# Four graph layers on one core: layer 0's weights as the stationary operand, layer 1 in a written order, one tile moved from matrix to list

## The chip, the core and the metric

The kernel runs on one core of a Trainium2 chip. The metric is the time on the device in microseconds (us). The core's engines work in parallel, each through its own queue in order: TensorE (PE, with its weight loads PEld), VectorE (DVE), ScalarE (ACT), GpSimd (POOL) and SyncE (SP). SBUF is the working memory of 128 partitions, PSUM the memory that matmuls write to.

## The reference, cut to what matters

There are B = 8 batches of N = 2048 nodes with D = 64 values each and one adjacency matrix of 2048 x 2048, in which a node has few neighbours. Four layers follow each other, each as `x = layernorm(x + layer(x, adj))`.

```python
# layer 0: attention with a score that is a sum of two parts
h = layernorm((x * nw + nb + x) @ W) * g0 + b0
e = leaky_relu(s1[:, :, None] + s2[:, None, :], 0.2)      # s1 = h.a1, s2 = h.a2
att = softmax(where(adj > 0, e, -big)); out = elu(att @ h + h)
# layer 1: a softmax over neighbours for each of the 64 values by itself
feat = softplus(x * w0 / sqrt(2) + b0); scores = feat * wa + ba
out[i] = sum_j adj exp(scores[j]) feat[j] / sum_j adj exp(scores[j])
# layer 2: mean over the neighbours, two weight matrices, relu, layernorm
# layer 3: four attention heads and an output head, layernorm
```

## The kernel before, in words

Nodes lie in NT = 16 tiles of 128; a tile holds a node's 8 x 64 values as one row of 512. The preparation (L360 to L425) reads the adjacency matrix tile by tile and makes two forms of it. For the first DENSE = 8 tiles of receiving nodes it makes the matrix `ET` in fp8, transposed by PE (L367 to L372). For all tiles it makes lists: `src`, the sending nodes of each edge in 5 windows of 128 edges for each of two groups of 64 nodes, and the selections `SelT` and `Sel`, which say which edge belongs to which node. `node_products` (L287) computes layer 0's products, normalises them into `H` and writes them to the table `htab0` in device memory. In `H` the first value of each batch is replaced by the neighbour's part of the score; it is recovered later from the fact that the values of a norm add to nothing (L494).

**Layer 0's loop** (L514 to L532) stands under a manual schedule: PE, ACT, DVE and POOL keep the order of the program. `fetch` issues ten indirect DMAs (gathers, L204) for a tile, each fetching the rows of 128 edges, and has PE bring the receiver's part of the score to the edges (`pe`, L451). `weights` adds both parts, takes the leaky maximum and two Exps. `weigh` multiplies the gathered rows by their weights on DVE (L472, five products of 128x1024), and PE adds them up with the selection as stationary operand (L478, 512 columns moving) and the weights beside them into `pd` (L480). `divide`, `combine`, `activate` and `normalise` follow one to three turns later.

**Layer 1** first makes its rows (`make_rows`, L571): exp(score) and its product with the feature, 1024 values per node, written to `rtab` (L587) and split in three bf16 pieces `R` (L589 to L593, on POOL, DVE, ACT and POOL). Tiles 0 to 7 are summed by matrix: `add_rows` (L598) multiplies `ET` by the pieces, six matmuls per pair of tiles (L601), the first FIRST = 3 tiles while the rows are made. Then tiles 15 down to 8 are summed by list: `fetch` (L637) gathers rows of 4 KB from `rtab`, `add_edges` (L646) sums them (L656), in three quads of four, four and two gathers per tile, spread between the matrix steps of tiles 3 to 7 by the condition at L672. `finish` (L607) divides (L610), adds to X and norms pairs of tiles. A planner orders what stands under no manual schedule.

**Layer 2** turns all rows (L803 to L821), then sums in the same two ways: matrix tiles with three matmuls per pair (L978), list tiles by gathers from `ytab` and L958, under a manual schedule with POOL copying finished tiles (`show`, L901). `by_list` and `by_matrix` follow DENSE (L796, L932), so the change reaches into this layer too. Layer 3 follows: the heads (gathers `xs`, weights at L1083) and the output head, which sums with weights as the stationary operand (L1420); both use lists alone and don't depend on DENSE.

Of the kernel before, what the change touches and what calls it, by code (L numbers as in the profile page):

```python
# [48 lines left out]
def kernel(ctx: ExitStack, tc: tile.TileContext, ins: dict, out: bass.AP):  # L49
# [150 lines left out]
    DENSE = 8  # L200
# [23 lines left out]
    htab0 = dram.tile([N + 1, BD], F32, name="htab0")  # L224
    no_row(htab0)
    l0 = ExitStack()
    wp = l0.enter_context(tc.tile_pool(name="l0w", bufs=1))
    H = wp.tile([P, NT, BD], F32, name="H")
# [33 lines left out]
    for k, a in enumerate((a1, a2)):  # L262
# [5 lines left out]
        if k:  # L268
            first_col = wp.tile([P, 2], F32, name="first_col")
            nc.vector.tensor_copy(first_col, Wv[:, :, 0])  # L270
            nc.vector.tensor_copy(Wv[:, :, 0], Wa[:, 1])
            nc.vector.tensor_copy(Wa[:, 1], first_col)

# [13 lines left out]
    def node_products(t0, wk, ps):  # L287
# [4 lines left out]
        for q in range(HALF):  # L292
# [14 lines left out]
            nc.vector.tensor_reduce(var[:, q], sq[:, :, 1:], AX.X, ALU.add)  # L307
            held.append(ph)
        v4, r4, t4 = (a.rearrange("p q (a k) -> p q a k", k=2) for a in (var, rstd, tmp))
        nc.vector.tensor_tensor(t4, pq[:, :, :, 1], pq[:, :, :, 1], ALU.mult)  # L310
        nc.vector.tensor_tensor(var, var, tmp, ALU.add)
        nc.vector.scalar_tensor_tensor(var, var, 1.0 / D, eps.unsqueeze(2).to_broadcast(var.shape), op0=ALU.mult, op1=ALU.add)
        inv_sqrt(*(a.rearrange("p q b -> p (q b)") for a in (rstd, var, tmp)))
        for q, ph in enumerate(held):
            t = t0 + q
            nc.vector.tensor_tensor(H[:, t].rearrange("p (b d) -> p b d", d=D),
                                    ph.rearrange("p a (k d) -> p (a k) d", d=D), along(rstd[:, q]), ALU.mult)
            nc.sync.dma_start(htab0[t * P:(t + 1) * P, :], H[:, t])
# [111 lines left out]

    wk = l0.enter_context(tc.tile_pool(name="l0k", bufs=2))
    ps_e = l0.enter_context(tc.tile_pool(name="l0pse", bufs=2, space=PSUM))
    ps_o = l0.enter_context(tc.tile_pool(name="l0pso", bufs=3, space=PSUM))
    ps_w = l0.enter_context(tc.tile_pool(name="l0psw", bufs=1, space=PSUM))
    held, zs, stats = {}, {}, {}

    def fetch(it):
        hs = wk.tile([P, GS * NG, B, D], F32, name="hs")
        for s in range(GS):
            for g in range(NG):  # L440
                gather(hs[:, s * NG + g].rearrange("p b d -> p (b d)"), htab0, it, s, g)
        selTf = wk.tile([P, GE], F32, name="selTf")
        nc.scalar.activation(selTf, SelT[:, it], AF.Copy)  # L443
        self_ = wk.tile([P, NG, NQ, GB], F32, name="self_")
        nc.scalar.activation(self_, Sel[:, it], AF.Copy)
        s1g = wk.tile([P, NG, B], F32, name="s1g")
        nc.vector.tensor_tensor(s1g, S1[:, it].unsqueeze(1).to_broadcast(s1g.shape),
                                group.unsqueeze(2).to_broadcast(s1g.shape), ALU.mult)
        pe = ps_e.tile([P, GS, NG * B], F32, name="pe")
        for s in range(GS):  # L450
            nc.tensor.matmul(pe[:, s], selTf[:, s * P:(s + 1) * P], s1g.rearrange("p g b -> p (g b)"), start=True, stop=True)  # L451
        held[it] = hs, self_, pe

    def weights(it):
        hs, self_, pe = held[it]
        wm = wk.tile([P, GS * NG, B], F32, name="wm")
        nc.vector.tensor_tensor(wm, pe.rearrange("p s (g b) -> p (s g) b", b=B), hs[:, :, :, 0], ALU.add)
        w = ps_w.tile([P, GS * NG, B], F32, name="w")
        nc.vector.scalar_tensor_tensor(w, wm, 0.2, wm, op0=ALU.mult, op1=ALU.max)
        nc.scalar.activation(wm, w, AF.Exp)  # L460
        nc.scalar.activation(w, w, AF.Exp)  # L461
        held[it] = hs, self_, w, wm

    def weigh(it):
        hs, self_, w, wm = held[it]
        po = ps_o.tile([P, BD], F32, name="po")
        pd = ps_w.tile([P, B], F32, name="pd")
        for n, ss in enumerate(TOGETHER):
            for s in ss:
                own = slice(s * NG, (s + 1) * NG)  # L470
                wx = hs[:, own].rearrange("p g b d -> p (g b) d")
                nc.vector.tensor_tensor(wx, wx, along(w[:, own].rearrange("p g b -> p (g b)")), ALU.mult)  # L472
            for s in ss:
                for g in range(NG):
                    for k, _, _ in blocks_of(s):
                        nodes = node_block(g, k)
                        first, last = n == 0, n == len(TOGETHER) - 1
                        nc.tensor.matmul(po[nodes], self_[:, g, QS.index((s, k))], hs[:, s * NG + g].rearrange("p b d -> p (b d)"),  # L478
                                         start=first, stop=last)
                        nc.tensor.matmul(pd[nodes], self_[:, g, QS.index((s, k))], wm[:, s * NG + g], start=first, stop=last)  # L480
        held[it] = po, pd

    def divide(it):
        po, pd = held.pop(it)
        rd = wk.tile([P, B], F32, name="rd")
        nc.vector.reciprocal(rd, pd)
        z = zs[it] = po.rearrange("p (b d) -> p b d", d=D)
        for b in range(B):
            nc.scalar.activation(z[:, b], z[:, b], AF.Copy, scale=rd[:, b:b + 1])

    def combine(it):
        z = zs[it]
# [1631 lines left out]
```

## Time and profile before

| What | us |
|---|---|
| median of 3 runs (lowest to highest) | 1791.36 (1789.67 to 1793.22) |
| the profiled execution | 1787.87 |
| its span, first to last instruction | 1785.6 |
| mean granted TensorE clock | 0.879 |
| first gather of layer 0 | 205.7 |
| last weights of layer 0 (L457) start | 420.66 |
| layer 1's first matmul (L601) | 466.47 |
| layer 2's first product (L808) | 720.98 |
| layer 2's first matrix matmul (L978) | 767.4 |
| first gather of layer 3's heads | 945.55 |

A line of the profile names a line of the kernel, the engine, the operation, output <- inputs with their shapes, and a count. In the groups the columns behind the bar are busy time in us, mean ns of one, and the idle time of the engine before them with what ended most of it; in the timeline a line begins with start and length in us, and brackets hold the wait before it and what ended it. The clock is the share of full speed granted to TensorE.

### The profile page before, as it was taken

The numbers are of one execution on the slowest core, as the hardware profiler recorded it, in microseconds if no ns is written. First come the engines' busy times: TensorE is split into PE (matmuls) and PEld (weight loads), VectorE is DVE, ScalarE is ACT, GpSimd is POOL, SyncE is SP. The second block draws the span as 40 slices with busy tenths as digits, with TensorE's granted clock in tenths as the row PEclk, the third lists the DMA queues.
The fourth block names the chain that finished last, engine by engine and source line by source line (L and its number), as shares of the span: only waits on it lengthen the run. The fifth ranks groups of instructions, "written<-read, shape, count | busy, mean of one in ns | idle before, by whom it ended". The sixth has DMA issues, their size and how long they took to land.

```text
span 1785.6 us, 38641 instructions
## 1 busy us (share of the span) xinstructions
PE 1380.7 (77%) x15230; PEld 946.5 (53%) x15264; DVE 1222.1 (68%) x2928; ACT 919.3 (51%) x1927; POOL 870.9 (49%) x820
## 2 busy tenths in 40 slices
PE   2663255463489998789757999999999986999993
PEld 2553133231133333633225877777777765878783
DVE  6889568988566656656583666666666654787787
ACT  4653225454972222635654565665655642567674
POOL 0000376762365552556625445455454524777761
PEclk9765567766599999899877999999999997999997
DMA  7422376662124885246624455555555536788771
GB/s 216 142 95 95 96 205 195 196 192 86 67 99 172 315 312 174 77 136 193 180 70 119 124 158 147 139 148 150 146 144 142 154 83 190 211 230 227 204 216 44
DMA packets 154135, 280.64 MB, mean 157 GB/s; under 512 B 64892, under 2 KB 91452, under 8 KB 151868
## 3 DMA queue, kind: packets, MB, share of 16 engines
q0 software_dynamic: 56320, 189.44, 35.3%
q1 hardware_dynamic: 80986, 84.45, 16.2%
q10 hardware_dynamic: 16640, 4.20, 1.0%
q8 instruction: 123, 2.02, 0.5%
q14 instruction: 66, 0.54, 0.1%
HBM read 237.60 MB, written 40.42 MB: 156 GB/s over the span
## 4 chain that ended last, share of the span: by engine, by line
PE 42%; DVE 13%; ACT 6%; issue 5%; POOL 3%; DMA 1%; DVEq 0%; SPq 0%; ACTq 0%; POOLq 0%
PE pscore L1077 7%; PE pa L601 6%; PE po L1099 5%; PE pt L1064 4%; PE pscore L1040 4%; PE pa L656 2%; PE ps L1381 2%; PE po L1420 2%; PE py L808 2%; DVE z L1152 2%; POOL hs L204 1%; PE pt L1358 1%; PE pa L978 1%; ACT z L845 1%; PE pscore L1162 1%
## 5 line engine op out<-in xcount | busy, mean ns | idle before, releaser
L204 POOL DMA_INDIRECT hs<-htab,src x160 | 153.1, 957 | 260.0 <-ACT selTf L443 201.1
L204 POOL DMA_INDIRECT xs<-xtab,src x160 | 207.0, 1293 | 114.7 <-PE po L1099 64.2
L1083 DVE SCALAR_TENSOR_TENSOR w<-w,Sel 128x640 f32<-128x640 f32 (+2 forms) x160 | 153.2, 957 | 135.4 <-ACT w L1080 134.4
L601 PE MATMUL pa<-R,ET 128*128 128x512 bf16 x746 | 179.5, 395 | 51.0 <-POOL R L589 35.5
L204 POOL DMA_INDIRECT hs<-ktab,src x160 | 158.4, 990 | 63.6 <-issue 36.0
L1077 PE MATMUL pscore<-U,xsT 64*128 64x80 f32 (+2 forms) x2560 | 183.0, 283 | 0.0
L1077 PEld LDWEIGHTS pscore<-U,xsT 64*128 64x128 f32 x2560 | 157.8, 190 | 43.5 <-ACT xsT L1066 22.7
L601 PEld LDWEIGHTS <-ET 128*128 128x128 fp8e4 x768 | 75.4, 101 | 163.6 <-issue 85.1
L170 ACT ACTIVATE X<-X,ln_m,ln_r 128x64 f32<-128x64 f32 x256 | 87.2, 427 | 138.8 <-DVE ln_m L162 138.8
L1066 ACT COPY xsT<-pt 128x512 f32<-128x512 f32 x160 | 93.6, 585 | 105.0 <-PE pt L1064 105.0
L1080 ACT ACTIVATE w<-pscore 128x640 f32<-128x640 f32 (+2 forms) x160 | 119.5, 747 | 46.6 <-PE pscore L1077 44.4
L1099 PE MATMUL po<-w,xs 128*64 128x88 f32 (+2 forms) x3072 | 139.0, 236 | 0.7 <-DVE w L1083 0.7
L1064 PE MATMUL pt<-ident,xs 128*128 128x128 f32 x640 | 106.8, 290 | 23.5 <-DMA xs<-xtab,src 22.9
L1099 PEld LDWEIGHTS po<-w,xs 128*64 128x64 f32 x3072 | 113.5, 137 | 14.9 <-DVE w L1083 0.9
L204 POOL DMA_INDIRECT rs<-rtab,src x80 | 75.9, 948 | 62.4 <-PE pa L656 42.6
L610 DVE RECIPROCAL rec<-pa 128x256 f32<-128x256 f32 x32 | 54.1, 1729 | 63.9 <-PE pa L656 38.0
L1381 PE MATMUL ps<-U,hsT 128*128 128x64 f32 x768 | 93.8, 269 | 1.5 <-ACT hsT L1359 1.5
L472 DVE TENSOR_TENSOR hs<-hs,w 128x1024 f32<-128x1024 f32 x80 | 91.8, 1213 | 3.1 <-ACT w L461 3.1
L1381 PEld LDWEIGHTS ps<-U,hsT 128*128 128x128 f32 x768 | 92.6, 192 | 1.9 <-ACT hsT L1359 1.7
L978 PE MATMUL pa<-Y,ET 128*128 128x512 bf16 x372 | 89.1, 386 | 3.1 <-DVE rest L818 2.1
L1468 ACT ACTIVATE z<-z,ln_m,ln_r 128x64 f32<-128x64 f32 x240 | 83.4, 431 | 15.3 <-DVE ln_m L1456 15.3
L204 POOL DMA_INDIRECT rs<-ytab,src x80 | 77.0, 963 | 26.9 <-issue 15.3
(632 smaller groups left out, 3053.8 us busy)
## 6 DMA issues: line engine op xcount, KB each, us to landing
at<-in_adj SPq DMA_DIRECT2D x16, 1024.0 KB
R<-itab SPq DMA_DIRECT2D x60, 256.0 KB
rtab<-r SPq DMA_DIRECT2D x16, 512.0 KB
ptab<-hp SPq DMA_DIRECT2D x16, 384.0 KB
hi<-ptab SPq DMA_DIRECT2D x16, 384.0 KB
ktab<-hb SPq DMA_DIRECT2D x16, 260.0 KB
X<-in_x ACTq DMA_DIRECT2D x16, 256.0 KB
htab<-H SPq DMA_DIRECT2D x16, 256.0 KB
```

The costliest lines, as they stand in the source:

```text
L170: nc.scalar.activation(v[:, b], v[:, b], AF.Identity, scale=rstd[:, k:k + 1], bias=nmr[:, k:k + 1])
L204: nc.gpsimd.indirect_dma_start(out=dst, out_offset=None, in_=table[:, :], in_offset=bass.IndirectOffsetOnAxis(ap=src[:, it, s, g:g + 1], a ...
L472: nc.vector.tensor_tensor(wx, wx, along(w[:, own].rearrange("p g b -> p (g b)")), ALU.mult)
L601: nc.tensor.matmul(po[h].rearrange("p a f -> p (a f)"), ET[:, jt, it * P:(it + 1) * P], R[:, jt, q, h].rearrange("p a f -> p (a f)"), star ...
L978: nc.tensor.matmul(sums[it], ET[:, jt, it * P:(it + 1) * P], Y[:, jt, q].rearrange("p a n -> p (a n)"), start=(jt == 0 and q == 0), stop=( ...
L1064: nc.tensor.transpose(pt[:, p], xss[k][:, p * P:(p + 1) * P], ident)
L1066: nc.scalar.copy(xsTs[k], pt)
L1077: nc.tensor.matmul(pscore[:, k_, f0:f0 + HN * ni].rearrange("p (h i) -> p h i", i=ni), xsT[half, p], Us[it][half, p, :, i0:i0 + ni], start ...
L1080: nc.scalar.activation(w.rearrange("p k a h i -> p k (a h i)"), pscore[:, :, 0:NP * HN * ni], AF.Exp)
L1083: nc.vector.scalar_tensor_tensor(wt, wt, 3.0e38, edge, op0=ALU.min, op1=ALU.mult)
L1099: nc.tensor.matmul(po[half, p, :, a - blk * GB:b - blk * GB], xs[:, f0:f0 + D], w[:, k_, p, :, a - WINDOWS[s][0]:b - WINDOWS[s][0]], start ...
L1381: nc.tensor.matmul(pscore[:, g, 2 * p:2 * p + 2], hsT[:, g, p], U[:, p, :, node_block(g, k)], start=False, stop=(p == NP - 1))
```

## The change

Layer 0: a row of `htab0` holds 66 values per batch: the neighbour's score, a one, and all 64 values. The weights are spread over the selection (`W`, on DVE) and become the stationary operand for each batch, window and block of nodes; the gathered rows move 65 columns at a time, so that the one gives the sum of the weights. Gathers come into half tiles (`hs`, five buffers). Layer 1's rows are made in layer 0's loop, behind the norms (`f` in `normalise`, `logits`, `row_out`), and only written to `rtab`. Layer 1 stands under a manual schedule as a whole: it reads the rows back (`load_rows`), splits them on ACT and DVE (`pieces`), issues the first gathers ahead of the first pieces and spreads the quads over all matrix steps; the statistics and the scaling of finished tiles come two and six steps later. DENSE is 7.

```diff
-    DENSE = 8
+    DENSE = 7
...
+    E0 = D + 2
+    htab0 = dram.tile([N + 1, B * E0], F32, name="htab0")
...
+    H = wp.tile([P, NT, B, E0], F32, name="H")
+    nc.gpsimd.memset(H[:, :, :, 1], 1.0)
...
-        nc.vector.tensor_tensor(t4, pq[:, :, :, 1], pq[:, :, :, 1], ALU.mult)
-        nc.vector.tensor_tensor(var, var, tmp, ALU.add)
...
+        nc.vector.tensor_tensor(H[:, t0:t0 + HALF, :, 0].rearrange("p q (a k) -> p q a k", k=2), pq[:, :, :, 1], r4, ALU.mult)
...
     def fetch(it):
+        hs = [wk.tile([P, GS, B, E0], F32, name="hs", bufs=5) for _ in range(NG)]
+        for g in range(NG):
+            for s in range(GS):
+                gather(hs[g][:, s].rearrange("p b e -> p (b e)"), htab0, it, s, g)
...
-        self_ = wk.tile([P, NG, NQ, GB], F32, name="self_")
-        nc.scalar.activation(self_, Sel[:, it], AF.Copy)
...
     def weights(it):
+        for g in range(NG):
+            nc.vector.tensor_tensor(wm[:, g], pe[:, 0, g], hs[g][:, :, :, 0], ALU.add)
+        nc.vector.scalar_tensor_tensor(wm, wm, 0.2, wm, op0=ALU.mult, op1=ALU.max)
+        nc.scalar.activation(pe[:, 1], wm, AF.Exp)
...
     def weigh(it):
+        for g in range(NG):
+            W = wk.tile([P, NQ, B, GB], F32, name="W", bufs=3)
+            for k in range(GN // GB):
+                of = [q for q, x in enumerate(QS) if x[1] == k]
...
+                nc.vector.tensor_tensor(W[:, of[0]:of[-1] + 1], Sel[:, it, g, of[0]:of[-1] + 1].unsqueeze(2).to_broadcast(shape),
+                                        pe[:, 1, g, ss[0]:ss[-1] + 1].unsqueeze(3).to_broadcast(shape), ALU.mult)
+            for n in range(NQ // 2):
+                for t in range(B):
+                    j, b = divmod(t, HB)
+                    for q in (n, n + NQ // 2):
+                        s, k = QS[q]
+                        nc.tensor.matmul(pv[node_block(g, k), j, b], W[:, q, t], hs[g][:, s, t, 1:], start=(n == 0 and b == 0),
+                                         stop=(n == NQ // 2 - 1 and b == HB - 1))
...
     def combine(it):
+        z = ps_w.tile([P, B, D], F32, name="z")
...
-        nc.vector.tensor_reduce(z[:, :, 0], z[:, :, 1:], AX.X, ALU.add, negate=True)
...
     def normalise(it):
+        f = fs[it] = rk.tile([P, B, D], F32, name="f")
+        nc.scalar.activation(f, X[:, it], AF.Exp, scale=w0, bias=bb)
+        if it % 2:
+            for t in (it - 1, it):
+                nc.scalar.activation(fs[t], fs[t], AF.Ln, bias=ones_col)
+
+    def logits(it):
+        nc.vector.tensor_tensor(e, fs[it].rearrange("p (h b) d -> p h b d", h=2), over(wa, e.shape), ALU.mult)
+        nc.scalar.activation(r[:, :, 0], r[:, :, 1], AF.Exp)
+
+    def row_out(it):
+        nc.vector.tensor_tensor(r[:, :, 1], fs.pop(it).rearrange("p (h b) d -> p h (b d)", h=2), r[:, :, 0], ALU.mult)
+        nc.sync.dma_start(rtab[it * P:(it + 1) * P, :], r.rearrange("p h a n -> p (h a n)"))
...
-        for k in range(NT + 3):
+        for k in range(NT + 5):
...
+            if 3 <= k <= NT + 2:
                 normalise(k - 3)
+            if k % 2 and k >= 5:
+                logits(k - 5)
+                logits(k - 4)
+            if k % 2 == 0 and k >= 6:
+                row_out(k - 6)
+                row_out(k - 5)
...
+        gk = l1.enter_context(tc.tile_pool(name="l1g", bufs=6))
...
+        def load_rows(jt):
+                rfs[jt] = wk.tile([P, 2 * BD], F32, name="rf")
+                nc.sync.dma_start(rfs[jt], rtab[jt * P:(jt + 1) * P, :])
+
+        def pieces(jt):
+                nc.scalar.copy(hi, rf)
+                nc.vector.tensor_tensor(rf, rf, hi, ALU.subtract)
+                nc.scalar.copy(mid, rf)
+                nc.vector.tensor_tensor(lo, rf, mid, ALU.subtract)
...
+                at_step(k + 2, take_stats, it & ~1)
+                at_step(k + 6, scale, it & ~1)
...
+        steps = [(it, jt) for jt in range(NT) for it in range(FIRST)] + [(it, jt) for it in range(FIRST, DENSE) for jt in range(NT)]
+        LATE, EARLY = 9, 4
+        with tc.manual_schedule(engines=engines):
+            load_rows(0)
+            load_rows(1)
+            fetch(0)
+            fetch(1)
+            pieces(0)
...
+            for k, (it, jt) in enumerate(steps):
+                if k % FIRST == 0 and k < NT * FIRST:
+                    pieces(jt + 2)
+                    load_rows(jt + 4)
...
+                add_rows(sums[it], it, jt)
+                if jt == NT - 1:
+                    finish(it, k)
+                while n < len(quads) and n * (len(steps) - LATE - EARLY) <= (k - LATE) * len(quads):
+                    add_edges(n)
+                    if quads[n][1] == len(TOGETHER) - 1:
+                        finish(quads[n][0], k)
+                    fetch(n + 2)
+                    n += 1
+                for f, a in later.pop(k, ()):
+                    f(*a)
```

## The prediction

> **What bounds the kernel now.** I read the busy time by stretches first, with cuts at the turns of the stages: layer 0's loop, its tail, layer 1's rows, layer 1's lists, the way into layer 2, layer 2. Columns: length, busy time of PE, PEld, DVE, ACT, POOL, granted clock, DMA share, GB/s.
>
> ```profile
> 205.70:420.66 214.96, 112.75 (x873) 66.59 (x872) 169.87 (x332) 92.35 (x281) 153.14 (x160) 0.70 0.67 196
> 420.66:466.47 45.81, 5.65 (x48) 2.87 (x49) 28.76 (x78) 28.64 (x71) 1.41 (x2) 0.59 0.03 8
> 466.47:551.10 84.63, 70.81 (x268) 29.08 (x274) 57.19 (x44) 60.16 (x68) 55.76 (x31) 0.86 0.24 96
> 551.10:705.30 154.20, 152.34 (x862) 56.60 (x877) 92.08 (x230) 36.55 (x104) 75.96 (x83) 1.00 0.77 273
> 705.30:720.98 15.68, 1.94 (x8) 1.59 (x9) 9.78 (x41) 11.28 (x34) 1.51 (x12) 0.62 0.14 30
> 768.00:945.50 177.50, 133.44 (x629) 48.18 (x638) 112.36 (x415) 89.88 (x244) 93.51 (x105) 0.87 0.50 143
> ```
>
> Each stretch has its own limit. The loop is held by DVE and by the gathers' issue. In the next 46 us nothing is full and PE does almost nothing. Then 274 matmuls take 85 us. From 551 PE is full at clock 1.00. Layer 2 is full of nothing: its chains pass from engine to engine. The costliest groups and the timeline give the prices.
>
> ```profile
> L204 POOL DMA_INDIRECT hs<-htab,src x160 | 153.1, 957 | 260.0 <-ACT selTf L443 201.1
> L204 POOL DMA_INDIRECT xs<-xtab,src x160 | 207.0, 1293 | 114.7 <-PE po L1099 64.2
> ```
> ```profile
> 330.48 2.31 PE L451 MATMUL pe<-s1g,selTf 128*128 128x16 f32 x10 [7.68 <-ACT selTf L443]
> 338.42 1.26 PE L451 MATMUL pe<-s1g,selTf 128*128 128x16 f32 x10
> ...
> 342.82 5.73 DVE L472 TENSOR_TENSOR hs<-hs,w 128x1024 f32<-128x1024 f32 x5
> ```
> ```profile
> 420.66 0.28 DVE L457 TENSOR_TENSOR wm<-pe,hs 128x80 f32<-128x80 f32 x1 [1.08 <-DMA hs<-htab,src]
> ...
> 466.47 0.58 PE L601 MATMUL pa<-R,ET 128*128 128x512 bf16 x1 [35.53 <-POOL R L589]
> ```
> ```profile
> 1605.61 0.69 DVE L1393 TENSOR_TENSOR w<-Sel,w_mid 128x512 f32<-128x512 fp8e4 x1 [0.43 <-ACT w_mid L1371]
> ...
> 1611.28 1.12 PE L1420 MATMUL po<-hs,w 128*32 128x65 f32 x32
> ```
>
> The reader sees a gather cost 0.96 us, the same ten small matmuls take 2.31 or 1.26 us (a factor of 1.83 by the clock), PE's 35.5 us wait before layer 1, and layer 3 already doing what layer 0 is to do.
>
> **The sum** is made against the profiled execution, 1787.87 us (span 1785.6 and 2.3 around it), 3.5 below the median of 1791.36.
>
> *Preparation, -1 us (-2 to 0).* One tile's 16 transposes and four ACT copies (4 x 0.60) go, beside a DVE that is over 90% busy and keeps its work but for two small operations per pair, 0.17 each.
>
> *Layer 0's loop, -3 us.* From the first L457 (220.96) to the sixteenth (420.66) are 15 turns of 13.3 us. A tile's ten gathers cost POOL 10 x (0.96 + 0.30) = 12.6, a floor that stays. DVE (12.0 busy per tile) loses the five products of L472 (5.7) and the reduction L494 (0.69), gains four products of 128x768 (0.88 each, between L1393's 0.69 for 512 and L472's 1.15 for 1024: 3.5), one add (0.25) and the two row products L584 and L586 (0.68 each): 10.7. ACT (7.2) loses a selection copy and an Exp (0.64), gains L576, L579 and L585 (0.74 + 0.64 + 0.58) and, per pair, two table loads of 1.28: 9.8. PE goes from 48 to 192 instructions for the sums, at L1420's 1.12/32 = 35 ns 6.7 us, at half clock 64 ns and 12.3. The loop's clock was 0.70, which would give 9.6 if it held; but a burst this long would start slow and end fast (the stretch at 84% PE had 0.86: 7.8), so I take 8. No engine is over 12.6, but a ring is close: two products (1.8) before PE may start, PE 8, the reciprocal (0.2) that waits for PE, three steps of combine (2.1) queued behind it on DVE and the next products behind those, 0.3 of handing over: 12.4; in every second turn the Exp of the weights stands behind two Ln and a table load on ACT, about 1 us. I take 13.1 per turn. Ends: POOL's 12.6 (-11) and 14.0 (+10). The DMAs of the rows (512 KB per tile, 40 GB/s) enter a stretch with a DMA share of 0.67 and 196 GB/s.
>
> Two of the new DVE operations per tile (L584's and L586's) read two SBUF tensors. In the heads stage, where L1083 does so, a gather takes 1.29 us on average against 0.96 here; should each of the two lengthen one gather by that 0.34, POOL's turn is 13.3, inside the ends. The Trainium skill's GPSIMD Engine Reference, section Specifications, says that GPSIMD shares its SBUF interfaces with VectorE and contends with DVE instructions that have two SBUF inputs; that rule speaks against the change. The trace agrees in the heads (1.29) but not each time: at 1601.5 us, beside L1398 (1.23, two SBUF tensors), a gather took 0.97.
>
> *The tail, +3.5 us (0 to 8).* From the last L457 to layer 1's first matmul are 45.8 us. After the change, in us behind that L457: adds, reciprocal and combine 3.0, PE done 12.8, tile 15 scaled on ACT behind two row Exps 19.2, combined 24.6, its Exp behind table loads and Ln 27.8, activation and statistics 33.3, 16 scalings and two Exps 41.5, Ln 44.1, Exp 46.6, product 47.4, then layer 1's first piece and a wait, 49.3. Rows are made early, but ACT and DVE keep program order, so layer 1's pieces stand behind the last row.
>
> *Layer 1, -31 us.* PE before: 466.5 to 705.3, 238.8 us. Where it is full, three steps (18 matmuls) take 3.99 us and a quad 1.85. After: 7 x 16 x 6 = 672 matmuls are 149 us, 27 quads 50, together 199. Warming up adds 2. The lists now start at step 9 instead of step 58, spread over the stage. What is late next is the feeding of the first 48 steps. Per row tile ACT needs two copies (1.04 each, L592) and DVE two subtractions (1.2, L591), 4.5 us in a row, about 3.5 if overlapped, against 4.0 of PE and 1.5 of quads; but `finish` (5 us on DVE, waiting for PE) and 16 scalings (5.4 on ACT) stand in the same queues, and `rf` has two buffers. I take 7 us of stalls: 208. Ends: none (-40), and the 24 us that PE lost in 466 to 551 (-14). Gathers need 90 x 1.26 = 113 us of POOL and are hidden; with six `rs` buffers the second four of a tile wait for half of the first, covered by 4 us of matrix steps.
>
> *Into layer 2, 0.* The last pair is again finished, measured and scaled in line: 5 + 4.2 + 5.4 + 1 = 15.6, as 15.7 now.
>
> *Layer 2, +3 us (-6 to 13).* A matrix tile is 48 matmuls, 10.8 us, a list tile 3.2, so PE saves 7. POOL gets ten gathers more, 12.6, and is the slower one already (12.6 per list tile against 11.4 of PE's share). But POOL also stands still for 25 us before the copies L904, waiting for ACT; with more gathers ahead of each copy most of that fills. Layer 3 is unchanged: 840 us.
>
> Sum: -1 - 3 + 3.5 - 31 + 3 = -28.5, that is 1759.4 on the profiled execution, 1763 as a median.
>
> **Rivals.**
>
> *Slower: the ring in layer 0 runs at half clock.* PE would be idle 4 us in each turn, and the loop's clock of 0.70 speaks for it; full-speed L1420 in a busy stage against. At 64 ns the burst is 12.3, the ring 16.7, the loop 15 x 3.6 = 54 us longer: 1817. It decides from 15.0 us per turn, a burst of 10.4, or 54 ns per instruction. The Trainium skill (TensorE: Matmul & The Clock Gate, section "HAM oscillation — how this bites in real kernels") says that idle gaps over about 3.4 us bring the clock back to half; by it each turn begins cold, and half of 3.4 us is lost: an estimate of 8.4 instead of 8 per burst, 6 us in the sum.
>
> *The feeding of layer 1 eats the gain.* The first 48 steps must move 16 rows and about 35 gathers of 0.52 MB, 27 MB, in 81 us: 330 GB/s, where the lists of now moved 273. At 273 they take 98 and stalls grow from 7 to 24: 1780.
>
> *Layer 2 pays all ten gathers.* Without the filling, +12.6 instead of +3: 1773. For it speaks POOL's unbroken issue from 797 to 841 us.
>
> *The rows come no earlier.* The tail above is this case, and it is in the forecast: what is gained is density in layer 1, not an earlier start.
>
> **Numbers.** Forecast 0.50, layer 1's feeding 0.18, layer 2's gathers 0.12, the slow ring 0.15, an even result between them 0.05. Taken to their ends together the terms give 1732 to 1808; ends in one direction are unlikely, so I give 1738 to 1795, leaving 0.05 below and 0.15 above. A measurement here tells about 0.2% (3.6 us) from no change: faster 0.80, same 0.05, slower 0.15.
>
> **What would show it.** Right: L457's sixteenth copy near 415 to 420 us in the trace, PE's burst per tile near 8 us, layer 1's first matmul 49 us later, its last about 208 us after that at a busy PE, and layer 2 from its first matrix step to the first head gather near 180. Wrong: turns over 15 us with the reciprocal waiting for PE; PE waiting in the first 48 steps for ACT's or DVE's pieces or for `rf`; PE waiting for gathers in either list; gathers well over 0.96 us beside the row products.

## The result, and the profile after

The kernel after takes 1811.28 us (median of 4 runs, 1808.23 to 1815.42) where the kernel before took 1791.26 beside it (4 runs): a ratio of 1.0113, 95% interval 1.009 to 1.0136. The forecast was 1763 (1738 to 1795). So the change makes the kernel 1.1% slower, where 1.6% faster had been forecast. Its profiled execution has a span of 1808.3 us, 22.7 more than before, at a mean clock of 0.883.

The view by stretches of the kernel after, cut at the turns of the stages as before (length; busy time of PE, PEld, DVE, ACT, POOL; granted clock, DMA share, GB/s):

```profile
204.20:411.80 207.60, 137.13 (x2922) 132.42 (x2924) 141.43 (x339) 117.54 (x294) 155.52 (x160) 0.73 0.79 231
411.80:466.19 54.39, 10.34 (x310) 9.98 (x305) 29.14 (x76) 36.24 (x75) 0.14 (x1) 0.63 0.25 96
466.19:594.00 127.81, 104.56 (x502) 37.00 (x512) 72.82 (x88) 38.87 (x51) 52.34 (x46) 0.91 0.71 239
594.00:720.10 126.10, 112.58 (x584) 40.60 (x592) 68.31 (x176) 35.36 (x103) 41.75 (x44) 0.96 0.58 191
720.10:781.10 61.00, 41.20 (x193) 33.38 (x192) 44.12 (x86) 31.12 (x63) 32.02 (x43) 0.92 0.23 78
781.10:966.00 184.90, 140.07 (x606) 46.07 (x618) 115.23 (x415) 91.11 (x246) 102.70 (x116) 0.90 0.53 151
```

Layer 0's loop ends 8.9 us earlier than before (411.8 for 420.7), and the tail behind it gives all of it back (54.4 for 45.8): PE starts layer 1 at the same moment. Then the two halves of layer 1 take 127.8 + 126.1 = 253.9 us where layer 1 took 238.8. Neither half is full of anything: PE is busy for 82% and 89% of the time, the DMAs at 0.71 and 0.58. So something stands in line. PE's waits in layer 1 (us in total, times, longest; the 40.2 are the tail before the first matmul):

```profile
PE pa L606 <- ACT R L595: 40.2, 1, 40.2
PE pa L658 <- ACT self__5520 L652: 9.1, 1, 9.1
PE pa L658 <- DMA rs<-rtab,src: 8.8, 8, 2.8
PE pa L658 <- ACT self__4843 L652: 6.5, 1, 6.5
PE pa L658 <- ACT self__4983 L652: 3.2, 1, 3.2
PE pa L658 <- ACT self__5154 L652: 3.2, 1, 3.2
PE pa L606 <- ACT R L597: 1.8, 1, 1.8
PE pa L606 <- DVE R L598: 1.6, 3, 0.7
```

The pieces of the rows (R), which the forecast feared, cost 3.4 us. Four copies of a selection (self_, L652), half a microsecond of ACT each, cost 22.0. How one of them comes to be late is read from three engines' timelines (start, length, and in brackets the wait before it):

```profile
510.11 1.92 PE L658 MATMUL pa<-rs,self__4843 128*32 128x512 f32 x16
511.97 4.06 PE L606 MATMUL pa<-R,ET 128*128 128x512 bf16 x17
519.20 1.92 PE L658 MATMUL pa<-rs,self__4983 128*32 128x512 f32 x16 [3.18 <-ACT self__4983 L652]
...
511.24 1.76 DVE L619 RECIPROCAL rec<-pa 128x256 f32<-128x256 f32 x1 [10.23 <-PE pa L658]
...
516.43 1.22 DVE L596 TENSOR_TENSOR rf<-rf,R 128x1024 f32<-128x1024 f32 x1
...
517.68 1.04 ACT L597 CAST R<-rf 128x1024 bf16<-128x1024 f32 x1 [16.38 <-DVE rf L596]
518.63 0.52 ACT L652 ACTIVATE self__4983<-Sel 128x384 f32<-128x384 fp8e4 x1
```

PE ends a list tile at 512. DVE has stood before that tile's `finish` for 10.2 us, with a subtraction of the next row tile queued behind it; ACT's cast waits for the subtraction (16.4), the small copy stands behind the cast, and PE, three matrix steps later, waits for the copy. It is a ring through three queues that keep their written order: PE waits for work that was queued behind something that waited for PE.

### The profile page after: what moved, and what is told of

It is laid out like the page before. It is cut to its first block, busy times and chain, and to the rows that moved or that the text cites. A ratio compares the mean times of both kernels' runs of the same rounds, so it can differ in the third digit from the quotient of the medians.

```text
span 1808.3 us, 43096 instructions
## 1 busy us (share of the span) xinstructions
PE 1412.7 (78%) x17448; PEld 1009.5 (56%) x17480; DVE 1189.7 (66%) x2917; ACT 922.6 (51%) x1907; POOL 844.4 (47%) x809
## 4 chain that ended last, share of the span: by engine, by line
PE 40%; DVE 14%; ACT 6%; DMA 5%; issue 5%; POOL 2%; SPq 0%; DVEq 0%; POOLq 0%; ACTq 0%
PE pscore L1095 7%; PE po L1117 5%; PE pt L1082 4%; PE pa L606 4%; PE pscore L1058 4%; PE ps L1399 3%; PE pa L658 2%; PE po L1438 2%; DMA rs<-rtab,src 2%; DMA rs<-ytab,src 2%; PE pt L1376 2%; DVE z L1170 2%; PE py L826 1%; DVE rec L619 1%; PE pa L996 1%
## 5 line engine op out<-in xcount | busy, mean ns | idle before, releaser
L204 POOL DMA_INDIRECT xs<-xtab,src x160 | 207.3, 1296 | 114.4 <-PE po L1117 62.7
L606 PE MATMUL pa<-R,ET 128*128 128x512 bf16 x652 | 153.1, 388 | 45.6 <-ACT R L595 40.2
L204 POOL DMA_INDIRECT rs<-rtab,src x90 | 94.2, 1047 | 198.9 <-PE pa L658 121.5
L1095 PE MATMUL pscore<-U,xsT 64*128 64x80 f32 (+2 forms) x2560 | 182.8, 283 | 0.0
L1095 PEld LDWEIGHTS pscore<-U,xsT 64*128 64x128 f32 x2560 | 157.6, 190 | 43.5 <-ACT xsT L1084 22.7
L489 PE MATMUL po<-hs,W 128*32 128x65 f32 x3072 | 121.1, 257 | 42.8 <-DVE W L482 22.6
L606 PEld LDWEIGHTS <-ET 128*128 128x128 fp8e4 x672 | 64.8, 100 | 146.6 <-issue 77.5
L489 PEld LDWEIGHTS po<-hs,W 128*32 128x32 f32 x3072 | 116.7, 136 | 45.9 <-DVE W L482 24.8
L204 POOL DMA_INDIRECT rs<-ytab,src x90 | 86.6, 962 | 29.6 <-issue 18.0
```

Of the source, the lines that this page charges most:

```text
L204: nc.gpsimd.indirect_dma_start(out=dst, out_offset=None, in_=table[:, :], in_offset=bass.IndirectOffsetOnAxis(ap=src[:, it, s, g:g + 1], a ...
L489: nc.tensor.matmul(pv[node_block(g, k), j, b], W[:, q, t], hs[g][:, s, t, 1:], start=(n == 0 and b == 0), stop=(n == NQ // 2 - 1 and b == ...
L606: nc.tensor.matmul(po[h].rearrange("p a f -> p (a f)"), ET[:, jt, it * P:(it + 1) * P], R[jt][:, q, h].rearrange("p a f -> p (a f)"), star ...
L1095: nc.tensor.matmul(pscore[:, k_, f0:f0 + HN * ni].rearrange("p (h i) -> p h i", i=ni), xsT[half, p], Us[it][half, p, :, i0:i0 + ni], start ...
```

## The experiments

By the record they ran on five chips (e1, e2, e4 and e6 on 13; e0, e8, e11 and e12 on 9; b0, x1 and e13 on 2; e14 on 0; e16 and e17 on 1). On all of them the kernel before itself takes 1888 to 1898 us instead of 1791, so their times are read as ratios to it, run beside them, and by stage. What differs there is shown under experiments 3 and 4; the chip of the first pair is not on record, so whether the chip is what makes the difference is not shown. b0 and x1 are one execution each, and every row of stages is one execution. This table is worked out from each run's profile, in us: from the first weights of layer 0 to the last (loop), to layer 1's first matmul (tail), to the start of its last (layer 1), to layer 2's first matrix step, to the first heads gather (layer 2), and the rest; ahead of these the span holds 209 to 222 us more. One thing makes the loop column unequal: with the old sums the first weights wait for all ten gathers of tile 0, with the new ones for five, and so they start 6.1 to 6.6 us sooner. Counted alike, from tile 0's complete scores to tile 15's, the loop of the kernel after is 192.4 us (199.7 before), that of e0 272.1 (219.6 in b0) and that of x1 182.8.

| Kernel | ratio to before (95%) | loop | tail | layer 1 | to layer 2 | layer 2 | rest | span |
|---|---|---|---|---|---|---|---|---|
| before, as shown first | | 199.7 | 45.8 | 238.3 | 62.6 | 178.1 | 840.1 | 1785.6 |
| after, as shown first | 1.0113 (1.009-1.0136) | 198.5 | 54.4 | 253.7 | 61.2 | 184.9 | 842.3 | 1808.3 |
| b0 before again | | 219.6 | 45.9 | 238.3 | 62.7 | 181.6 | 916.4 | 1886.2 |
| e0 after again | 1.0420 (1.0345-1.0496) | 278.7 | 53.6 | 251.5 | 59.5 | 203.0 | 915.7 | 1977.1 |
| e1 copies early | 1.0348 (1.0302-1.0394) | 271.7 | 55.0 | 230.8 | 60.8 | 199.4 | 909.7 | 1944.5 |
| e2 eight by matrix | 1.0473 (1.0425-1.0521) | 275.3 | 54.5 | 266.6 | 59.4 | 184.9 | 916.4 | 1966.2 |
| e4 layer 0 alone | 1.0229 (1.0174-1.0284) | 275.0 | 45.5 | 238.8 | 61.7 | 184.4 | 919.3 | 1936.8 |
| e6 free order | 1.0374 (1.0318-1.0431) | 270.8 | 54.3 | 238.0 | 61.3 | 202.2 | 917.1 | 1957.6 |
| e8 early, 7 buffers | 1.0262 (1.0197-1.0327) | 278.8 | 53.6 | 222.6 | 59.6 | 204.1 | 919.4 | 1951.5 |
| e11 lists late | 1.0265 (1.0192-1.0338) | 279.7 | 54.9 | 228.2 | 59.8 | 203.8 | 919.2 | 1959.1 |
| e12 old sums | 1.0023 (0.9995-1.0051) | 225.0 | 54.6 | 222.1 | 60.6 | 203.6 | 920.8 | 1907.3 |
| x1 no gathers | | 189.1 | 54.6 | 253.3 | 60.4 | 199.5 | 921.0 | 1896.0 |
| e13 old sums, 8 | 0.9997 (0.9979-1.0016) | 222.4 | 54.7 | 230.4 | 60.4 | 184.9 | 916.6 | 1888.2 |
| e14 two pools | 0.9951 (0.9932-0.9969) | 223.1 | 32.9 | 244.5 | 60.5 | 185.2 | 912.7 | 1878.2 |
| e16 new sums, free pieces | 1.0209 (1.0182-1.0235) | 279.0 | 31.1 | 228.3 | 59.5 | 204.6 | 914.7 | 1931.1 |
| e17 old sums, free pieces | 0.9907 (0.9890-0.9923) | 224.9 | 33.0 | 244.0 | 59.3 | 183.7 | 913.1 | 1877.7 |

The theories: **A**, the written order makes PE wait for small copies; **B**, seven tiles by matrix cost their ten gathers; **C**, the read-back and the gathers are limited by bytes; **D**, layer 0's new sums are themselves no gain.

### 1. The copies one list tile earlier (e1), and no written order at all (e6)

```diff
+        def select(it):
+            if it >= DENSE:
+                selfs[it] = wk.tile([P, NG, NQ, GB], F32, name="self_")
+                nc.scalar.activation(selfs[it], Sel[:, it], AF.Copy)
...
             if c == 0:
-                selfs[it] = wk.tile([P, NG, NQ, GB], F32, name="self_")
-                nc.scalar.activation(selfs[it], Sel[:, it], AF.Copy)
                 sums[it] = new_sums()
...
             fetch(1)
+            select(NT - 1)
             pieces(0)
...
                     add_edges(n)
+                    if quads[n][1] == 0:
+                        select(quads[n][0] - 1)
```

> The kernel after, with each list tile's copy of its selection (L652) written one list tile ahead. Theory A (PE waits for small copies that stand in ACT's written order behind pieces, scalings and DVE's finish): the four waits of 6.5, 3.2, 3.2 and 9.1 us go, 22 us, and the matmuls at half clock after them, some 3; a part comes back as waits for gathers or pieces, 5. Layer 1 from 254 to about 234, the whole 1791 (1785 to 1798). Rival B (seven tiles by matrix, ten gathers more in layers 1 and 2) and rival C (read-back of the rows and gathers limit the first 48 steps by bytes): PE then waits as long for something else, and the time stays over 1805.

PE's waits in layer 1 of this kernel:

```profile
PE pa L661 <- DMA rs<-rtab,src: 10.2, 8, 2.8
PE pa L606 <- ACT R L597: 2.4, 2, 1.3
PE pa L661 <- issue: 2.4, 1, 2.4
PE pa L606 <- DVE R L598: 1.0, 2, 0.7
```

No wait for a copy is left, and layer 1 takes 230.8 us, 22.9 less than in the kernel after and 20.7 less than in its repetition. That is A's 22 us; C falls, since the same bytes now go through in less time. The repetition (e0) has the same four waits for copies as the kernel after (9.6, 6.7, 3.2 and 3.2 us), so layer 1 can be compared with both. What remains are eight waits for gathers. The total of 1791 that was expected can't be read here, as the next experiments show.

```diff
-        with tc.manual_schedule(engines=engines):
+        with ExitStack():
             load_rows(0)
```

> The kernel after, without the written order in layer 1: the same instructions and buffers, but their order on each engine is left to the program's planner, as before. Theory A (the written order makes the waits): the copies and pieces move ahead of DVE's finish and PE's 22 us of waits for the copies shrink to under 8: 1795 or below. Rival C (the rows' read-back and pieces cannot come faster than 4 us per tile, whatever the order): within 5 us of 1811.

Layer 1 takes 238.0 us, 15.7 less, without a wait for a copy: order alone, with the same work and buffers (13.5 less than in e0). In its place PE waits 14.2 us for gathers, so the planner's order is not as good as the corrected written one.

### 2. Eight tiles by matrix (e2)

```diff
-    DENSE = 7
+    DENSE = 8
...
-        ga = wp.tile([P, D], F32, name=f"ga{k}")
+        ga = aw.tile([P, D], F32, name=f"ga{k}")
```

> The kernel after, with eight tiles by matrix instead of seven (two small constants move to another pool for the room). Rival B: the ten gathers go out of layers 1 and 2, 12.6 us of POOL each, and the time falls to 1797 or below. Theory A: layer 1 gets 96 matmuls more (21 us) and 3 quads less (5.6), the waits for the copies stay, since the order is the same: layer 1 up by 8 to 16, layer 2 down by 7: 1812 to 1820.

Layer 1 is 15.1 us longer than in e0 and has its waits for copies (the longest 15.8); layer 2 is 18.1 shorter. The two about cancel and the intervals of the ratios overlap: B is a real price in layer 2 (on these chips, more than the expected 7), but not what made the change slower.

### 3. Layer 0's new sums alone (e4), both kernels again (b0, e0)

The edit, against the kernel after: layer 0 as there without `logits` and `row_out`, layer 1 as in the kernel before.

```diff
-        for k in range(NT + 5):
+        for k in range(NT + 3):
...
-            if k % 2 and k >= 5:
-                logits(k - 5)
-                logits(k - 4)
```

> Layer 0 in its new form (weights as stationary operand, ones in the rows), but layer 1 wholly as before: rows made there, order as before, eight tiles by matrix. Theory A: layer 0's new form is a gain, 7 to 11 us in its loop down to POOL's floor of 12.6 per turn and 1 before it, nothing given back: 1782 (1778 to 1786). Rival D (the new form of the sums is itself what costs, by its longer PE bursts at a low clock): 1791 or over.

The ratio is 1.0229 and the loop has 275 us, where the execution shown first had 198.5. D holds on these chips; it does not in the first pair, where the new loop, counted alike, is 7.3 us shorter. The tail is 45.5 again, so the tail's 8 us do not belong to the sums but to what e4 leaves out: the rows made behind the norms and layer 1's new order and memory. Both kernels were then run unchanged:

> The kernel after, unchanged, on the chip of this set: the first experiments fell on a chip on which the kernel before itself took 1890 us and in which PE's long runs of short matmuls show gaps without a visible cause (69 us of them in layer 0's sums, 27 in layer 3's). If that is a property of the chip, the kernel after has a loop of layer 0 of about 270 us there and a ratio of 1.04 to 1.05; on a chip without it, a loop of 198 and a ratio of 1.011. Layer 1 takes 254 us on either.

> The kernel before, unchanged, for its stages on these chips. If PE's gaps come only with long runs of short matmuls beside gathers, its layer 0 (48 wide and 48 narrow matmuls per tile instead of 192) has a loop of 200 to 212 us here too, layer 3 takes about 362 us instead of 296 as in all runs on these chips, layer 2 about 185; layer 1 stays at 238. If the gaps hit every gather stage alike, layer 0's loop is 225 or over.

The kernel after has a loop of 278.7 and a ratio of 1.042, the kernel before a loop of 219.6, between the two ends expected. Layer 3's output head, alike in all, takes 358 to 367 us from its first gather to the end in every run here, where it took 296 and 298. PE's timeline in layer 0's last turns, of the kernel after again:

```profile
475.35 2.98 PE L489 MATMUL po<-hs,W 128*32 128x65 f32 x103 [0.55 <-issue]
478.51 0.35 PE L489 MATMUL po<-hs,W 128*32 128x65 f32 x4 [0.18 <-issue]
479.30 0.29 PE L489 MATMUL po<-hs,W 128*32 128x65 f32 x2 [0.44 <-issue]
480.02 0.34 PE L489 MATMUL po<-hs,W 128*32 128x65 f32 x5 [0.44 <-issue]
480.80 0.26 PE L489 MATMUL po<-hs,W 128*32 128x65 f32 x2 [0.43 <-issue]
...
489.56 6.66 PE L489 MATMUL po<-hs,W 128*32 128x65 f32 x190 [0.42 <-DVE W L482]
```

"issue" is a pause for nothing that the profile shows. Two to five matmuls, a pause of 0.4 us, again every 0.75 us: the tile that began at 471 takes 14.3 us. The next, from 489, runs through in 7.5. Between them POOL issued the last gather, at 482.7. The sum of these pauses of PE in layer 0's products (us in total, times, longest), first in the kernel after as shown first, then in its repetition:

```profile
PE po L489 <- issue: 20.3, 8, 5.2
PE po L489 <- issue: 90.9, 125, 15.9
```

The eight of the first line stand ahead of a tile's products, none within them.

### 4. The same sums without gathers (x1)

```diff
-        hs = [wk.tile([P, GS, B, E0], F32, name="hs", bufs=5) for _ in range(NG)]
+        hs = first[0] if it else [wk.tile([P, GS, B, E0], F32, name="hs", bufs=5) for _ in range(NG)]
         for g in range(NG):
-            for s in range(GS):
+            for s in range(GS if it == 0 else 0):
```

> The kernel after, with layer 0's gathers of tiles 1 to 15 left out: every tile uses the ten row sets of tile 0 with the ones written once, so the result of layer 0 is not the reference's. If PE's gaps in layer 0's sums come from the gathers' traffic, they vanish, a tile's 192 matmuls take 7 to 8 us as in the last two tiles, and the turn falls to the ring of the prediction without POOL's floor: 10 to 12.4 us, a loop of 150 to 186. If the gaps belong to PE's instruction supply alone, they stay: a loop of 230 or over.

```profile
298.80 6.73 PE L493 MATMUL po<-hs,W 128*32 128x65 f32 x192
306.41 1.29 PE L461 MATMUL pe<-s1g,selTf 128*128 128x16 f32 x10 [0.87 <-ACT selTf L455]
309.04 0.40 PE L493 MATMUL po<-hs,W 128*32 128x65 f32 x2 [1.34 <-DVE W L486]
309.82 7.94 PE L493 MATMUL po<-hs,W 128*32 128x65 f32 x190 [0.38 <-DVE W L486]
```

The same matmuls without gathers: no pause, 6.3 to 8.8 us per tile, a loop of 189.1, or 182.8 counted alike: 12.2 per turn, inside the 10 to 12.4 expected. This execution has the slowness all the same: in its output head, whose gathers were left in, PE pauses 44 times (27.2 us in all) where the first pair shows no such row. So layer 0's pauses need the gathers beside them. Whether it is their traffic or POOL's issuing of them is not told apart, since x1 leaves out both; and why the first pair had none within its products beside 231 GB/s, no run here shows.

### 5. Seven buffers (e8), and later lists (e11)

```diff
-        gk = l1.enter_context(tc.tile_pool(name="l1g", bufs=6))
+        gk = l1.enter_context(tc.tile_pool(name="l1g", bufs=7))
...
-        R = {jt: wp.tile([P, 3, 2, 2, HB * D], BF16, name=f"R{jt}") for jt in reversed(range(NT))}
+        R = {jt: wp.tile([P, 3, 2, 2, HB * D], BF16, name=f"R{jt}") for jt in range(NT)}
```

> The kernel after with the copies of the selections written one list tile ahead, seven buffers for the gathered rows instead of six, and the row pieces of layer 1 laid out in rising order in memory. Theory A: layer 1 from 254 us to 231 by the copies, as measured, and by another 6 to 10 by the seventh buffer (PE's eight waits for gathers, 10 us, mostly go): 221 to 225. If the wait of 4.5 us before the first piece is for memory that the last row still holds, the tail goes from 54 to 50. Together 28 to 37 us less than the kernel after. Rival C (the waits for gathers are of bytes, not of buffers): layer 1 stays at 229 or over.

```profile
PE pa L661 <- issue: 5.5, 1, 5.5
PE pa L606 <- ACT R L597: 3.5, 2, 1.7
PE pa L661 <- DVE X L622: 2.3, 2, 1.6
PE pa L606 <- DVE R L598: 1.6, 3, 0.7
PE pa L606 <- issue: 1.1, 7, 0.2
PE pa L661 <- DMA rs<-rtab,src: 1.0, 1, 1.0
```

One more buffer of 4 KB per partition takes PE's waits for gathers from 10.2 to 1.0 us and layer 1 to 222.6, as expected. (The rising order of the rows went in with it, so the buffer's share is read from these waits.) The Trainium skill (Perfetto Trace Analysis, section "Optimization Strategy") says that a gap that repeats on the engine that should be busy can mean too few buffers for the next tile; this is such a case. The second half of the expectation failed: with the rows in rising order the tail is the same (53.6), and ACT still stands 4.3 us before its first piece.

```diff
-        LATE, EARLY = 9, 4
+        LATE, EARLY = 40, 4
```

> As the kernel with early copies, seven buffers and rising order, but the lists start at step 40 instead of step 9, so that rows' read-back and gathers don't meet in the first 48 steps. If what is left there is the meeting of the two (rows waiting 19 us for their read-back beside gathers): the first 48 steps take 16 times 4 us, 64 to 68, the rest 138 to 142, layer 1 202 to 210. If the pieces' own chain (4 us per row tile) and POOL's 113 us for the gathers decide, the lists' work only moves: 220 or over.

The first 41 steps, free of lists, took 62 us (548 to 610), 1.51 each where a full PE takes 1.33; 48 at that rate are 73, not 64 to 68, and the other 166 us of layer 1 hold 145 of work. Layer 1 took 228.2, the second case: keeping the lists out of the first steps moves their work, it saves none.

### 6. The old sums with the rest (e12, e13)

```diff
-        hs = [wk.tile([P, GS, B, E0], F32, name="hs", bufs=5) for _ in range(NG)]
+        hs = wk.tile([P, GS * NG, B, D], F32, name="hs")
...
-                        nc.tensor.matmul(pv[node_block(g, k), j, b], W[:, q, t], hs[g][:, s, t, 1:], start=(n == 0 and b == 0),
-                                         stop=(n == NQ // 2 - 1 and b == HB - 1))
+                        nc.tensor.matmul(po[nodes], self_[:, g, QS.index((s, k))], hs[:, s * NG + g].rearrange("p b d -> p (b d)"),
+                                         start=first, stop=last)
```

> Layer 0's sums as in the kernel before (values scaled, the selection stationary), layer 1's rows made behind layer 0's norms and layer 1 as in the kernel with early copies, seven buffers and rising order; seven tiles by matrix. DVE then carries 12.0 us of the old products and 1.4 of the rows per tile, over POOL's 12.6: a loop of 202 to 212 us on any chip, also where short matmuls are issued slowly. On a chip without that slowness it is 5 to 10 us slower than the kernel with early copies and the new sums; on one with it, 50 to 65 us faster.

> As the kernel with the old sums in layer 0, rows behind its norms, early copies, seven buffers, but eight tiles by matrix. Rival B said that the ten gathers cost: on these chips layer 2 falls from 204 to 185. Layer 1 gets 96 matmuls (21 us) for 3 quads (5.7): from 222 to 234 to 238. Together 3 to 7 us less than with seven tiles, a ratio of 0.998 to 1.001 to the kernel before. Should layer 1's lists have been the bound with seven tiles, it stays under 230 and the ratio is 0.996 or less.

The old sums take 225.0 us with the rows behind them (202 to 212 had been expected; the kernel before alone has 219.6 here), 54 less than the new ones of e8 on these chips, 47 counted alike. Why they take 219.6 and 225.0 here and 199.7 in the first pair was not followed further. With eight tiles layer 2 falls from 203.6 to 184.9 and layer 1 rises by 8.3, less than the 12 to 16 expected: 0.9997, no difference to be told. Layer 1 has been won back by then (230.4 for 238.3); the tail (54.7 for 45.9) eats it.

### 7. What the first piece waits for (e14)

```diff
+        we = l1.enter_context(tc.tile_pool(name="l1e", bufs=1))
...
-        R = {jt: wp.tile([P, 3, 2, 2, HB * D], BF16, name=f"R{jt}") for jt in range(NT)}
+        R = {jt: (we if jt < 4 else wp).tile([P, 3, 2, 2, HB * D], BF16, name=f"R{jt}") for jt in range(NT)}
```

> As the kernel with the old sums, rows behind the norms, early copies, seven buffers and eight tiles by matrix, but the pieces of row tiles 0 to 3 in a pool of their own that lies over memory of layer 0's sums alone, not over the pool of the rows. If the 4.3 us that ACT waits before the first piece are for the pool that the last row still leaves by DMA (taken as a whole: with six-buffer layout and with rising order the wait was the same), the tail falls from 54.7 to 50.4 and the ratio to the kernel before to 0.996 to 0.999. If the wait is of another kind (the last row's write itself, or an order between the stages), the tail stays at 54 to 55 and the ratio at 1.000.

The tail falls to 32.9 us, by 21.8 where 4.3 had been expected. ACT's timeline in it, with PE's first matmul of layer 1, shows why:

```profile
470.80 1.03 ACT L603 CAST R<-rf 128x1024 bf16<-128x1024 f32 x1
471.85 1.28 ACT L516 ACT_TABLE_LOAD   x1
473.14 0.58 ACT L516 ACTIVATE e<-po 128x512 f32<-128x512 f32 x1
475.32 1.86 PE L614 MATMUL pa<-R,ET 128*128 128x512 bf16 x4 [22.65 <-DVE X L522]
...
481.07 1.05 ACT L603 CAST R<-rf 128x1024 bf16<-128x1024 f32 x1 [0.90 <-DMA rf<-rtab]
482.31 2.76 ACT L170 ACTIVATE X<-X,ln_m,ln_r 128x64 f32<-128x64 f32 x8 [0.19 <-DVE ln_m L162]
484.97 1.03 ACT L605 CAST R<-rf 128x1024 bf16<-128x1024 f32 x1
485.91 0.81 ACT L533 ACTIVATE f<-X,bb,w 128x512 f32<-128x512 f32 x1
...
496.95 1.15 ACT L542 ACTIVATE r<-r 128x512 f32<-128x512 f32 x2
503.12 1.04 ACT L603 CAST R<-rf 128x1024 bf16<-128x1024 f32 x1 [5.02 <-DMA rtab<-r]
```

The casts of layer 1's first pieces (L603, L605) now stand between layer 0's last scalings and Exps, and PE begins 20.5 us earlier, at 475.3. By the profile its wait now ends on DVE's L522, layer 0's last reading of its sums in PSUM, so the pieces are no longer what its first matmul waits for. The wait for the last row's DMA, 5.0 us, has moved to the fifth row tile, the first one in the pool that lies over layer 0's rows. So it was that pool as a whole that held the first piece, and with it the pieces' place in ACT's queue. Against its set's runs of before the kernel is half a per cent faster, 0.9951, by an interval that leaves out 1; part of the 21.8 us comes back, as layer 1 stretches to 244.5: PE reaches the first list at step 9 before the last row is in memory and waits 12.2 us for gathers, 10.3 of them at once.

### 8. All three put right (e16, e17)

```diff
         wp = l1.enter_context(tc.tile_pool(name="l1w", bufs=1))
-        wk = l1.enter_context(tc.tile_pool(name="l1k", bufs=2))
         gk = l1.enter_context(tc.tile_pool(name="l1g", bufs=7))
+        wk = l1.enter_context(tc.tile_pool(name="l1k", bufs=2))
+        we = l1.enter_context(tc.tile_pool(name="l1e", bufs=1))
...
-        R = {jt: wp.tile([P, 3, 2, 2, HB * D], BF16, name=f"R{jt}") for jt in range(NT)}
+        R = {jt: (we if jt < 10 else wp).tile([P, 3, 2, 2, HB * D], BF16, name=f"R{jt}") for jt in range(NT)}
...
-        LATE, EARLY = 9, 4
+        LATE, EARLY = 18, 4
```

> The change's own parts kept (new sums in layer 0, rows behind its norms, written order, seven tiles by matrix), with early copies, seven buffers, and the memory of layer 1 laid out so that the pieces of row tiles 0 to 9 and the gathered rows of the lists have pools of their own and only row tiles 10 to 15 lie over layer 0's constants; the lists start at step 18. From the last weights of layer 0 to the last matmul of layer 1 the forecast had 49.3 + 208 = 257; the kernel after took 305 on these chips, the one with early copies and seven buffers 276. If the pool was the last thing that held it back, about 255 to 262. If DVE and ACT, shared with the last rows, are the next bound, 265 to 272. Layer 0's loop stays at 270 to 280 on these chips, so the whole stays over the kernel before (1.013 to 1.022).

> The same layout and start of the lists with the old sums in layer 0 and eight tiles by matrix. From the last weights to the last matmul of layer 1 the kernel with two pools took 277.4, 11.8 of it in waits of PE for the first gathers at step 9, which could not start before the last row was written. If these and the 5.0 us before the fifth row's pieces go: 260 to 266, the ratio to the kernel before 0.987 to 0.991. If the pieces of later rows are the next bound: 270 to 275 and 0.992 to 0.995.

The diff is against e8 and gives e16. With the change's own parts, tail and layer 1 take 31.1 + 228.3 = 259.4 us, inside the 255 to 262 expected; in the kernel after again they took 305.1. With the old sums the two stages take 277.0, outside both expectations and the same as with two pools (277.4): PE's waits for the first gathers went from 12.2 to 2.1 us, but it then waited 6.9 for DVE's `finish` (L630) and 3.7 for nothing shown. The total is the best of all, 0.9907, inside the first expectation and under both kernels on these chips, but not for the reason that was given. That it is below e14's 0.9951 is not explained by the two profiles, whose spans are 0.5 us apart (e14's nine times reach from 1877 to 1893 us, and the profile caught one of the shortest).

## Why the prediction was wrong, point by point

**Layer 1 is the step that failed**: "I take 7 us of stalls: 208." It holds 46 of the 51 us between the forecast and the measured execution: 31 us less than before had been forecast, 15 more were measured. The work was right (from start to start three steps take 3.98 us at full clock and a quad 1.86, 199 us as forecast); what came on top was 55 us, not the 2 of warming up and 7 of stalls. The selection copies made 21 to 23 of them (taken away in e1) and the missing seventh buffer 8 (e8). The other 24 no run has taken away; in e8 they are 6.6 us of pauses for nothing shown, 5.6 of waits for pieces, 2.7 for `finish`, 1.0 for gathers, and some 8 of matmuls under the full clock (0.96 on average). The forecast had named the queues ("`finish` ... and 16 scalings ... stand in the same queues") but looked for their price at the pieces and at `rf`, and never at the copy L652, a half-microsecond instruction that nothing hid once order was fixed. Of the six buffers it said "covered by 4 us of matrix steps"; but the next fetch waits for PE to end the quad (POOL waited for PE's quads 26 times), and eight times it was late.

**The tail** was costed at 49.3 and took 54.4; the wait of 4.5 us on "DMA rtab<-r", which the sum did not have, is most of the difference. The reason given for it, "ACT and DVE keep program order, so layer 1's pieces stand behind the last row", fell with e14: they stand there because their pool lies over that of the rows. With another pool they come in between and the tail is 33.

**Layer 0** was right within its terms. Counted alike, the start came 1.5 us earlier (1 forecast) and the loop took 12.8 us per turn where 13.1 had been forecast, 7.3 less than before in all instead of 3. PE's burst was put at 8 us; over the first 14 tiles it is 6.8 to 9.0, 7.9 on average, at granted clocks of 0.64 to 0.80. That it fits is partly luck: the 8 came from 6.7 at full clock, and where x1 shows such a burst at clock 1.00 it is busy for 5.8, so the price of one matmul was too high and the clock taken too high as well. The estimate by the Trainium skill (TensorE: Matmul & The Clock Gate, section "HAM oscillation — how this bites in real kernels") was 8.4; the tiles at a clock of 0.64 to 0.67 took 7.9 to 9.0, the others 6.8 to 8.2, so on average the measurement is under it. Gathers took 0.972 us on average for 0.957 before; two lengthened by 0.34 per turn would have made it 1.03. The rival in which PE's ring is slow (54 us, given 0.15) has no part in the result, and that 1811 lies near its 1817 is chance. On the chips of the experiments its price came true, 52.5 us counted alike (e0 to b0), but by pauses beside the gathers and not by the clock, which is 0.71 to 0.74 in nearly all of e0's tiles.

**Layer 2**: +3 forecast, +6.8 measured in the first pair, inside the range; +21 on the other chips, over the 12.6 of the rival. POOL's stand before the copies L904, of which most was to fill, was 26.4 us in the first 147 us of the stage (15.9 of it ended by ACT, 10.5 by nothing shown) and is 18.5 after the change: about a third filled. **Layer 3 and the way into layer 2** stayed within 2.2 us.

**The rival "feeding of layer 1"** had the right stage, less than half the price (24 us of stalls) and the wrong cause: bytes. The DMAs were at 0.71 and 239 GB/s in the stretch, and e1 moved the same bytes 23 us faster. No rival had the written order itself as a cause, and the range ended at 1795, though its terms taken to their ends together reached 1808.

An estimate, from stage lengths only: the kernel after with experiment 8's repairs would lose 305.1 - 259.4 = 45.7 us, 1766 for 1811 where PE has no pauses. It wasn't run there.

## What to carry to other kernels

When an order is fixed by hand, follow for each small producer (a cast, a copy, a selection) what stands ahead of it on its own engine, and what that waits for; if the chain leads back to the engine that will wait, write the producer one tile earlier. Ask of every new pool over which old pool it lies and who leaves that last. Count buffers by what is in flight between two releases, and move a stage's sums to many short matmuls only after looking at how they run beside the transfers they will meet.

## What the hardware showed that was not expected

- Long runs of short matmuls (128x32 weights, 65 columns) can pause without a visible cause while gathers are in flight: 0.4 us in every 0.75 us in places, 14.3 us for 192 of them against 7.5 in the next tile and 6.3 to 8.8 without gathers. In the first pair the same instructions took 6.8 to 9.0 beside the gathers.
- After a wait of a few microseconds PE can pay twice: the sixteen matmuls of a quad behind the 6.5 us wait took 3.64 us at a granted clock of 0.50; behind a 3.18 us wait they took 1.92 once (519 us, clock 1.00) and 3.38 once (548 us, clock 0.55).
- DVE's reciprocal of 128x256 values from PSUM takes 1.75 us, a product of that size 0.43: two thirds of a `finish` of 5.2 us are its two reciprocals.
